# Layer 1's input of the next image loaded during layer 3, and its products and norms through single PSUM banks

## The chip, the cores and the metric

The kernel runs on one core of a Trainium2 chip, in one launch. The metric is the device time of that core in microseconds. The core has a matrix engine (TensorE, "PE" in the profile, whose weight loads are listed apart as "PEld"), a vector engine (VectorE, "DVE"), a scalar engine (ScalarE, "ACT"), a general engine (GpSimd, "POOL") and SyncE ("SP"), which issues DMA transfers. Matmul results go to PSUM, eight banks of 128 x 512 floats. All else that is worked on lies in SBUF. All data are fp32.

## The reference

Four images of 32 x 32 pixels (1024 tokens) with 384 channels pass through four residual layers, each after a group norm over 32 groups of 12 channels:

```python
x = x + layer0(gn(x)); x = x + layer1(gn(x)); x = x + layer2(gn(x)); x = x + layer3(gn(x))

# layer 0: deformable attention: q = x @ w_q, offsets by a grouped 3x3 convolution,
#   tokens sampled at shifted places, 6 heads of 64 with a sampled bias
# layer 1: attention with 12 heads of 32, weighted by how alike two tokens' groups are
qkv = x @ Wqkv                                       # -> q, k, v per head
xg  = x @ Wg + bg
gc  = depthwise_conv_3x3_stride2(xg, Wconv) + bconv  # 256 group centres
sim = sigmoid(beta + alpha * l2norm(xg_h) @ l2norm(gc).T)
group_weight = (sim @ sim.T) * gamma + (1 - gamma)
attn = softmax(q @ k.T * scale) * group_weight
attn = attn / (attn.sum(axis=2) + 1e-8)
out  = (attn @ v) @ Wproj
# layer 2: box sums over 5 columns and 20 channels, num / denum
# layer 3: outlook attention: v = x @ Wv; softmax over 9 for each of 9 window places of x @ Wa;
#   the weighted 3x3 patches are added back at their places
```

## The kernel before

An image is held channel-major: three tiles of 128 channels by 1024 tokens (`KC` = 3, `N` = 1024, `P` = 128; `NJ` = 8 blocks of 128 tokens). Layer 0 of an image is "the front" (class `Front`), layers 1 to 3 are "the trunk" (class `Trunk`, `image`). The front of image 1 runs alone. Then the trunk of image 1 runs beside the front of image 2 and so on, and the trunk of image 4 runs alone again. Both are generators: each `yield` gives a weight, and `Net.layer3` takes the next piece of the front whenever the front's share of work is less than 0.1 ahead of the trunk's. This sets the order in which the program is written; the order on each engine follows from a list scheduler when the kernel is built, and it is fixed then. Between front and trunk an image passes through DRAM (`self.x1`).

PSUM is split in two pools that front and trunk share: two "big" buffers of two banks (128 x 1024) and four single "bank" buffers (128 x 512). SBUF tiles come from pools with scopes: the tiles of a scope are given back at its end. Weights of 384 x 384 pass through a ring of three buffers (`weights`), loaded on SP's DMA queue, gmat (the group norm's averaging matrix) among them.

The places that the change touches, with the lines of the kernel before:

- `norm` (L309 to L357): the statistics of x on DVE (L306, L307), 14 matmuls with gmat that average the means (L330, from `gn_mv`), a few small DVE instructions, 14 matmuls for the deviations (L330, from `gn_d`), a square root, and three DVE instructions that write the normed x (L357).
- `inputs1` (L848 to L973), layer 1 up to its first head pair. It loads x (L852), norms it into xh, and makes three products with Wg (`dense_t`, L376, into a big buffer; bias on ACT, nine taps of the strided convolution on DVE). Then come the products for queries and keys (`queries_keys`, L885 to L893, six products into big buffers: queries evacuated by ACT, keys by DVE at L892, both stored to DRAM), the head norms (squares on ACT, matmuls with `hsum` L920, square root, reciprocal on DVE L934, broadcast back by `hall` matmuls at L947 into a big and a bank buffer, multiplied at L955 and L961) and the value products (`dense_n`, L390, a bank each, copied by ACT L899). Between these stand the eight steps of `sums_step` for the first pair: four matmuls (L1035) into both big buffers, a maximum on DVE (L1043) and an exponential with row sum on ACT (L1044), once for each of two heads. `sums_finish` (L1050 to L1063) takes the logarithm, transposes it and writes it to DRAM, from where `load_lse` brings it to a row of the query tile.
- `sims` (L1065 to L1087): eight matmuls (L1074) and four sigmoids (L1081) into a tile `sim`. `pair` then runs over eight blocks: POOL scales a block of sim (L1139), PE makes logits (L1154), ACT takes their exponential (L1162), and so on. In later pairs the sums of the following pair are made inside this loop.
- `layers23` and `layer2`: x comes back from DRAM on ACT's queue (L1227), and the denominators of layer 2 lie in three tiles `d`.
- The end of `layer3` (L1433 to L1481): for each of eight token blocks a row of DRAM is written (L1449) and read back shifted as `mt` (L1451), four on SP's queue and four on ACT's. PE meanwhile makes the last four value tiles (L390 from xh) and transposes x (24 transposes, L1460, three into each big buffer), which ACT copies into eight tiles y (L1464). Then come 22 products of `mt` and `vals` (L1472), the sum with y on DVE and the stores on SP (L1481).
- The front's instructions that stand around this place: its query product (L376 from `a`), the evacuation to `qpad` (L565), the convolution (L584) and, later, the indirect gathers that POOL issues (L652).

Of the kernel before, what the change touches and what calls it, by code (L numbers as in the profile page):

```python
# [26 lines left out]
P = 128  # L27
# [45 lines left out]
class Net:  # L73


    def __init__(self, ctx, tc, a):
        self.tc, self.nc, self.a = tc, tc.nc, a
        nc = self.nc
        pool = lambda name, bufs, **kw: ctx.enter_context(
            tc.tile_pool(name=name, bufs=bufs, **kw)  # L80
        )
        self.const = pool("const", 1)
        self.wts = pool("wts", 3)
        self.ps2 = pool("ps2", 2, space=PSUM)
        self.ps1 = pool("ps1", 4, space=PSUM)
        self.dram = pool("dram", 1, space=DRAM)
        self.n = 0
        self.consts()
        self.scratch()
        self.front, self.trunk = Front(self, "right"), Trunk(self, "left")  # L90

# [188 lines left out]
class Lane:  # L280
# [33 lines left out]
    def norm(self, x, out, mv=None):  # L314
# [7 lines left out]
        gmat = self.weights("gmat")  # L322
# [502 lines left out]
class Trunk(Lane):  # L825


    def image(self, b, out):
        with self.scope("l1y"):
# [18 lines left out]
    def inputs1(self, b):  # L848
        nc, v = self.nc, self.nc.vector
        x = self.wt([P, KC, N], "x")  # L850
        for k in range(KC):
            nc.sync.dma_start(x[:, k, :], self.x1[b % 2][k * P : (k + 1) * P, :])  # L852
        xh = self.wt([P, KC, N], "xh")
        self.norm(x, xh)
        yield 15

# [28 lines left out]
        def queries_keys(ko):  # L885
            for w, dst in ((wq, self.qd), (wk, self.kd)):
                ps = self.dense_t(w, xh, ko)
                t = self.wt([P, N], "qk", 2)
                if dst is self.qd:
                    nc.scalar.mul(t, ps, HD1**-0.5)  # L890
                else:
                    v.tensor_copy(t, ps)  # L892
                nc.sync.dma_start(dst[ko * P : (ko + 1) * P, :], t)  # L893
# [9 lines left out]
        queries_keys(0)  # L903
# [25 lines left out]
        queries_keys(1)  # L929
        yield 14  # L930
        wv = self.weights("Wqkv", 2 * C)
# [4 lines left out]
        queries_keys(2)  # L936
        yield 14
        self.sums_step(1, st)
        yield 10
        values(range(NJ // 2))  # L940
        self.sums_step(2, st)
        yield 18
        for k in range(KC):
            rows, heads = slice(k * P, (k + 1) * P), slice(32 * k, 32 * k + 32)
            ps, pc = self.big(), self.bank()
            for out, lo in ((ps[:, 0:512], 0), (ps[:, 512:N], 512), (pc[:, 0:M1], N)):
                nc.tensor.matmul(  # L947
                    out,
                    self.hall[heads, :],
                    inv[heads, lo : lo + out.shape[-1]],  # L950
                    start=True,
                    stop=True,
                )
            t = self.wt([P, N + M1], "sq", 2)
            v.tensor_tensor(  # L955
                t[:, 0:N].rearrange("p (y x) -> p y x", y=HW),
                pads[k][:, 1:, 1:],
                ps.rearrange("p (y x) -> p y x", y=HW),
                ALU.mult,
            )  # L960
            v.tensor_tensor(t[:, N:], raw[:, k, :], pc[:, 0:M1], ALU.mult)  # L961
# [4 lines left out]
            self.sums_step(3 + k, st)  # L966
            yield 8
        for i in range(2):
            values(range(4 + 2 * i, 6 + 2 * i))
            self.sums_step(6 + i, st)  # L970
        self.sums_finish(0, st)
        self.load_lse(0)
        yield 28  # L973
# [91 lines left out]
    def sims(self, p):  # L1065

        nc = self.nc
        sim = self.wt([P, 2, 2, N], "sim")
# [148 lines left out]
    def layers23(self, b, out):  # L1217
        with self.scope("l23"):
            self.x = self.wt([P, KC, N], "x")
# [36 lines left out]
    def layer2(self):  # L1256
        nc, v = self.nc, self.nc.vector
        with self.scope("l2"):
# [8 lines left out]
            def squares(k):  # L1267
# [24 lines left out]
                d = self.wt([P, HW, HW], "d", KC)  # L1292
# [61 lines left out]
    def layer3(self, b, out):  # L1354
        nc, v = self.nc, self.nc.vector
        skew = self.skew[b % 2]
        with self.scope("l3"):
# [98 lines left out]
            ys = []  # L1456
            for i in range(NJ):
# [5 lines left out]
                y = self.wt([P, C], "y", NJ)  # L1463
                nc.scalar.copy(y, pt[:, 0:C])  # L1464
                ys.append(y)
            yield 20
            for i in range(NJ):
# [11 lines left out]
                y = ys[i]  # L1479
# [87 lines left out]
```

## Time and profile before

| | |
|---|---|
| time, median of 3 runs | 4876.06 us (4868.23 to 4881.34) |
| the profiled execution's own time | 4831.1 us |
| its span, first to last instruction | 4829.3 us |
| granted TensorE clock, mean | 0.91 |
| front of image 1, alone | 0 to 637 us |
| trunk of images 1, 2, 3, 4 | 637 to 1829, to 2970, to 4055, to the end |
| PE, DVE, ACT, POOL busy | 87%, 65%, 50%, 20% |

The trunk's bounds are read from the last L1472 product of each image. The busy shares are means over stages that differ, so the stages that the change touches have to be read by themselves. PEclk is the mean clock that TensorE was granted in a stretch, as a share of full speed. The profile is of one execution and some 45 us below the median of the timed runs.

### The profile page before, as it was taken

To read this page: it belongs to the slowest core of one execution; us is meant where nothing else is said; L and a number is where in the kernel's file an instruction comes from. 1 tells how busy PE (TensorE), PEld (TensorE's weight loads), DVE (VectorE), ACT (ScalarE), POOL (GpSimd) and SP (SyncE) were. 2 spreads that over 40 slices of the span, in tenths; PEclk is the share of its full clock that TensorE was granted. 3 is DMA by queue.
4 is the path that set the end of the run, shared out by engine and by line. 5 is a ranking of instruction groups with operands and counts; after the bars stand their busy time and mean duration, and the time that the engine had idled before them with its cause. 6 is when DMAs were issued, how large, how long until landed. Compare 5 with 4: busy or idle time off the path is not lost.

```text
span 4829.3 us, 46659 instructions
## 1 busy us (share of the span) xinstructions
PE 4189.8 (87%) x15704; PEld 1799.4 (37%) x15704; DVE 3132.9 (65%) x5727; ACT 2404.9 (50%) x3693; POOL 946.3 (20%) x946
## 2 busy tenths in 40 slices
PE   5466678899999989889999989899999998999998
PEld 2222233333333353333333444343333335343444
DVE  3478828676877836577777762767687873454544
ACT  2155414565766513376666532457576641456642
POOL 1533303211212101421211210422121210000000
PEclk7677788999999989899999989799999998899998
DMA  6323244311212143431221224532121213201011
GB/s 118 102 84 92 70 131 144 94 53 38 80 50 73 36 147 105 126 86 50 60 62 54 65 76 113 154 92 56 33 80 42 75 45 114 87 23 33 19 39 40
DMA packets 230927, 366.82 MB, mean 76 GB/s; under 512 B 117475, under 2 KB 164672, under 8 KB 230688
## 3 DMA queue, kind: packets, MB, share of 16 engines
q1 hardware_dynamic: 169672, 197.36, 14.0%
q0 software_dynamic: 39936, 145.53, 10.3%
q10 hardware_dynamic: 21080, 20.96, 1.8%
q8 instruction: 124, 2.03, 0.2%
q14 instruction: 115, 0.94, 0.1%
HBM read 285.84 MB, written 78.21 MB: 75 GB/s over the span
## 4 chain that ended last, share of the span: by engine, by line
PE 35%; ACT 9%; DVE 7%; issue 3%; DMA 2%; POOL 0%; SPq 0%; ACTq 0%; DVEq 0%; POOLq 0%
PE bank L1184 8%; PE big L1154 4%; PE big L376 3%; PE big L1035 3%; PE bank L790 3%; PE bank L390 2%; PE bank L755 2%; PE bank L1128 2%; ACT big L1044 2%; PE bank L1179 2%; DVE e L1193 1%; DVE nmax L1043 1%; ACT e L1162 1%; PE big L1074 1%; PE bank L1472 1%
## 5 line engine op out<-in xcount | busy, mean ns | idle before, releaser
L1193 DVE SCALAR_TENSOR_TENSOR e<-bank,gam,e 128x512 f32<-128x512 f32 x768 | 557.6, 748 | 564.9 <-ACT gn L1192 275.1
L1184 PE MATMUL bank<-sim,sg 128*128 128x512 f32 (+3 forms) x2304 | 870.6, 512 | 2.8 <-DVE e L1193 2.8
L1044 ACT ACTIVATE big<-big,nmax 128x1024 f32<-128x1024 f32 x384 | 418.5, 1090 | 384.5 <-DVE nmax L1043 384.0
L734 POOL DMA_INDIRECT win<-strips,widx x384 | 425.8, 1109 | 887.4 <-DVE z L747 450.3
L1162 ACT ACTIVATE e<-big 128x1024 f32<-128x1024 f32 x384 | 376.8, 1019 | 360.2 <-PE big L1154 355.0
L1184 PEld LDWEIGHTS bank<-sim,sg 128*128 128x128 f32 x2304 | 405.9, 199 | 378.1 <-issue 297.7
L1043 DVE TENSOR_REDUCE nmax<-big 128x1 f32<-128x1024 f32 x384 | 453.1, 1217 | 54.4 <-PE big L1035 53.0
L1154 PE MATMUL big<-qa,ka 64*128 64x512 f32 x1536 | 412.1, 627 | 15.5 <-ACT big L1044 9.4
L1139 POOL TENSOR_SCALAR sg<-sim,gam 128x512 f32<-128x512 f32 x192 | 147.3, 770 | 1416.5 <-PE bank L1184 1126.9
L1035 PE MATMUL big<-k,q 32*128 32x512 f32 x1536 | 357.6, 701 | 74.5 <-ACT e L1162 37.0
L790 PE MATMUL bank<-lg,va 128*64 128x512 f32 x768 | 374.1, 634 | 44.7 <-ACT lg L788 44.6
L755 PE MATMUL bank<-qpad,kz 128*128 128x512 f32 x768 | 375.8, 620 | 22.6 <-DVE e L1193 13.7
L790 PE MATMUL bank<-lg,ones 128*64 128x512 f32 x768 | 373.4, 634 | 0.0
L746 ACT ACTIVATE z<-win,bias_f 128x528 f32<-128x528 f32 x384 | 277.0, 737 | 188.8 <-DVE lg L752 108.6
L752 DVE SCALAR_TENSOR_TENSOR lg<-z,bias_f,lg 128x512 f32<-128x512 f32 x384 | 299.9, 795 | 45.5 <-ACT lg L751 43.9
L747 DVE SCALAR_TENSOR_TENSOR z<-win,bias_f,z 128x528 f32<-128x528 f32 x384 | 291.8, 779 | 38.5 <-ACT z L746 38.1
L652 POOL DMA_INDIRECT gat<-pairs,sidx x192 | 210.8, 1098 | 448.1 <-DVE ix_gt L464 244.5
L751 ACT ACTIVATE lg<-z,bias_f 128x512 f32<-128x512 f32 x384 | 267.5, 719 | 44.1 <-DVE z L747 27.2
L787 DVE TENSOR_TENSOR lg<-lg,tb 128x512 f32<-128x512 f32 x384 | 246.2, 698 | 64.7 <-ACT tb L780 64.7
L756 DVE TENSOR_TENSOR lg<-bank,lg 128x512 f32<-128x512 f32 x384 | 256.3, 683 | 32.0 <-PE bank L755 30.7
L788 ACT ACTIVATE lg<-lg 128x512 f32<-128x512 f32 x384 | 222.4, 629 | 40.2 <-DVE lg L787 39.8
L1154 PEld LDWEIGHTS big<-qa,ka 64*128 64x128 f32 x1536 | 134.7, 188 | 272.0 <-issue 156.8
(262 smaller groups left out, 5812.2 us busy)
## 6 DMA issues: line engine op xcount, KB each, us to landing
pairs<-xn SPq DMA_DIRECT2D x64, 192.0 KB
q<-qd SPq DMA_DIRECT2D x48, 256.0 KB
w<-in_gmat SPq DMA_DIRECT2D x16, 576.0 KB
w<-in_w_off SPq DMA_DIRECT2D x12, 576.0 KB
w<-in_Wqkv SPq DMA_DIRECT2D x12, 576.0 KB
a<-in_x SPq DMA_DIRECT2D x16, 384.0 KB
x<-a ACTq DMA_DIRECT2D x4, 1536.0 KB
k<-a SPq DMA_DIRECT2D x12, 512.0 KB
```

Of the source, the lines that this page charges most:

```text
L734: nc.gpsimd.indirect_dma_start(out=win, out_offset=None, in_=self.strips[:, :], in_offset=bass.IndirectOffsetOnAxis(ap=self.widx[:, q, c : ...
L747: v.scalar_tensor_tensor(z, wv[:, 1 : HH + 1, 0 : HW + 1], sc(0, 1), z, ALU.mult, ALU.add)
L752: v.scalar_tensor_tensor(lg, z[:, :, 1 : HW + 1], sc(0, 0), lg, ALU.mult, ALU.add)
L755: nc.tensor.matmul(ps, kz[:, j * P : (j + 1) * P], both, start=True, stop=True)
L790: nc.tensor.matmul(po[out, :], w, lf, start=j == 0, stop=j == NJ - 1)
L1035: nc.tensor.matmul(ps[r][:, h * 512 : (h + 1) * 512], self.q4[rows, i * P : (i + 1) * P], self.k4[rows, 0:512], start=True, stop=True,)
L1043: v.tensor_reduce(nmax[:, r, i : i + 1], ps[r], AX.X, ALU.max, negate=True)
L1044: nc.scalar.activation(ps[r], ps[r], AF.Exp, bias=nmax[:, r, i : i + 1], accum_out=den[:, r, i : i + 1],)
L1154: nc.tensor.matmul(ps[:, r, :], ka[rows, j * P : (j + 1) * P], qa[rows, cols], start=True, stop=True,)
L1162: nc.scalar.activation(e, ps, AF.Exp)
L1184: nc.tensor.matmul(ps[:, (mid - i0) * P :], sg[:, r, m, :], sim[:, r, m, mid * P : i1 * P], start=m == 0, stop=m == 1,)
L1193: v.scalar_tensor_tensor(e[:, r, :], ps, self.gam[:, 1:2], e[:, r, :], ALU.add, ALU.mult, accum_out=tot[:, r, h : h + 1],)
```

## The change

The trunk gets a pool "keep" with one buffer of 128 x 4096 floats. `whole` hands it out: three quarters as x of an image, or all of it as the tile of `sims`, or three quarters as x of layers 2 and 3 and the fourth quarter as the third tile `d` of layer 2.

`start(b)` issues the loads of x and of gmat. For image 1 it is called at the head of `image`; for the others it is called in layer 3 of the image before, after the transposes of x (the buffer's last readers) and before the products with mt. The norm stands at the head of `image` and writes over x in place.

In layer 3 the eight tiles y are replaced by one tile that takes the place of xh, under the same tag.

`queries_keys` becomes `product`: each product is made in two halves, each in a bank, and evacuated by halves. The broadcast norms go through banks too, by 256, 512 and 512 columns. The order is rewritten: one product after each of the first sums steps, the sums steps 3 to 5 ahead of the norm of the same k, one value tile after each of the steps 3 to 7, the last three after `sums_finish`; the weights of the values are asked for later.

```diff
@@ -88,6 +88,7 @@
         self.consts()
         self.scratch()
         self.front, self.trunk = Front(self, "right"), Trunk(self, "left")
+        self.trunk.work = self.trunk.keep = pool("keep", 1, side="left")
 
     def nm(self, base):
         self.n += 1
@@ -311,7 +312,7 @@
         self.stat = self.work
         return self.wt([P, KC, 2], "gn_mv", 2)
 
-    def norm(self, x, out, mv=None):
+    def norm(self, x, out, mv=None, gmat=None):
 
 
         nc = self.nc
@@ -319,7 +320,8 @@
             mv = self.moments()
             for k in range(KC):
                 self.stats(mv, x, k)
-        gmat = self.weights("gmat")
+        if gmat is None:
+            gmat = self.weights("gmat")
 
         near = [[k for k in range(KC) if abs(k - ko) <= 1] for ko in range(KC)]
 
@@ -825,7 +827,28 @@
 class Trunk(Lane):
 
 
+    def whole(self):
+
+
+        work, self.work = self.work, self.keep
+        t = self.wt([P, 4 * N], "whole")
+        self.work = work
+        return t, t[:, 0 : KC * N].rearrange("p (k n) -> p k n", k=KC)
+
+    def start(self, b):
+
+        x = self.whole()[1]
+        for k in range(KC):
+            self.nc.sync.dma_start(x[:, k, :], self.x1[b % 2][k * P : (k + 1) * P, :])
+        self.begun = x, self.weights("gmat")
+
     def image(self, b, out):
+        if b == 0:
+            self.start(b)
+        x, gmat = self.begun
+        self.norm(x, x, None, gmat)
+        self.xh = x
+        yield 15
         with self.scope("l1y"):
 
 
@@ -847,13 +870,7 @@
 
     def inputs1(self, b):
         nc, v = self.nc, self.nc.vector
-        x = self.wt([P, KC, N], "x")
-        for k in range(KC):
-            nc.sync.dma_start(x[:, k, :], self.x1[b % 2][k * P : (k + 1) * P, :])
-        xh = self.wt([P, KC, N], "xh")
-        self.norm(x, xh)
-        yield 15
-
+        xh = self.xh
 
         pads, raw = [], self.wt([P, KC, M1], "raw")
         w = self.weights("Wg")
@@ -882,15 +899,24 @@
 
         wq, wk = self.weights("Wqkv"), self.weights("Wqkv", C)
 
-        def queries_keys(ko):
-            for w, dst in ((wq, self.qd), (wk, self.kd)):
-                ps = self.dense_t(w, xh, ko)
-                t = self.wt([P, N], "qk", 2)
+        def product(w, ko, dst):
+
+            t = self.wt([P, N], "qk", 2)
+            for h in range(2):
+                ps, out = self.bank(), t[:, h * 512 : (h + 1) * 512]
+                for ki in range(KC):
+                    nc.tensor.matmul(
+                        ps,
+                        w[:, ki, ko * P : (ko + 1) * P],
+                        xh[:, ki, h * 512 : (h + 1) * 512],
+                        start=ki == 0,
+                        stop=ki == KC - 1,
+                    )
                 if dst is self.qd:
-                    nc.scalar.mul(t, ps, HD1**-0.5)
+                    nc.scalar.mul(out, ps, HD1**-0.5)
                 else:
-                    v.tensor_copy(t, ps)
-                nc.sync.dma_start(dst[ko * P : (ko + 1) * P, :], t)
+                    v.tensor_copy(out, ps)
+            nc.sync.dma_start(dst[ko * P : (ko + 1) * P, :], t)
 
         def values(js):
             for j in js:
@@ -900,7 +926,9 @@
                 nc.sync.dma_start(self.vd[j * P : (j + 1) * P, :], t)
 
 
-        queries_keys(0)
+
+        product(wq, 0, self.qd)
+        product(wk, 0, self.kd)
         self.load_sums(0)
         self.load_pair(0)
         st = self.sums_state()
@@ -926,50 +954,49 @@
                 )
         nc.scalar.activation(inv[:, 0:N], psx[0 : KC * 32, :], AF.Sqrt)
         nc.scalar.activation(inv[:, N:], psc[0 : KC * 32, 0:M1], AF.Sqrt)
-        queries_keys(1)
+        product(wq, 1, self.qd)
         yield 14
-        wv = self.weights("Wqkv", 2 * C)
         for part in (inv[:, 0:512], inv[:, 512:]):
             v.tensor_scalar(part, part, 1e-12, None, ALU.max)
             v.reciprocal(part, part)
         self.sums_step(0, st)
-        queries_keys(2)
+        product(wk, 1, self.kd)
         yield 14
         self.sums_step(1, st)
-        yield 10
-        values(range(NJ // 2))
+        product(wq, 2, self.qd)
+        wv = self.weights("Wqkv", 2 * C)
+        yield 14
         self.sums_step(2, st)
-        yield 18
+        product(wk, 2, self.kd)
+        yield 14
         for k in range(KC):
+            self.sums_step(3 + k, st)
             rows, heads = slice(k * P, (k + 1) * P), slice(32 * k, 32 * k + 32)
-            ps, pc = self.big(), self.bank()
-            for out, lo in ((ps[:, 0:512], 0), (ps[:, 512:N], 512), (pc[:, 0:M1], N)):
+            t = self.wt([P, N + M1], "sq", 2)
+            parts = [(N, M1, raw[:, k, :], t[:, N:])]
+            for h in range(2):
+                out = t[:, h * 512 : (h + 1) * 512].rearrange("p (y x) -> p y x", x=HW)
+                parts.append((h * 512, 512, pads[k][:, 1 + 16 * h : 17 + 16 * h, 1:], out))
+            for at, n, src, out in parts:
+                ps = self.bank()[:, 0:n]
                 nc.tensor.matmul(
-                    out,
-                    self.hall[heads, :],
-                    inv[heads, lo : lo + out.shape[-1]],
-                    start=True,
-                    stop=True,
-                )
-            t = self.wt([P, N + M1], "sq", 2)
-            v.tensor_tensor(
-                t[:, 0:N].rearrange("p (y x) -> p y x", y=HW),
-                pads[k][:, 1:, 1:],
-                ps.rearrange("p (y x) -> p y x", y=HW),
-                ALU.mult,
-            )
-            v.tensor_tensor(t[:, N:], raw[:, k, :], pc[:, 0:M1], ALU.mult)
+                    ps, self.hall[heads, :], inv[heads, at : at + n], start=True, stop=True
+                )
+                if at < N:
+                    ps = ps.rearrange("p (y x) -> p y x", x=HW)
+                v.tensor_tensor(out, src, ps, ALU.mult)
             nc.sync.dma_start(self.xgd[rows, :], t[:, 0:N])
             nc.sync.dma_start(self.gcd[rows, :], t[:, N:])
             if k == 0:
                 self.load_groups(0)
-            self.sums_step(3 + k, st)
+            values(range(k, k + 1))
             yield 8
         for i in range(2):
-            values(range(4 + 2 * i, 6 + 2 * i))
             self.sums_step(6 + i, st)
+            values(range(3 + i, 4 + i))
         self.sums_finish(0, st)
         self.load_lse(0)
+        values(range(5, NJ))
         yield 28
 
     def pair_tiles(self):
@@ -1065,7 +1092,7 @@
     def sims(self, p):
 
         nc = self.nc
-        sim = self.wt([P, 2, 2, N], "sim")
+        sim = self.whole()[0].rearrange("p (r m n) -> p r m n", r=2, m=2)
         for h in range(2):
             for m in range(2):
                 ps = self.big().rearrange("p (r n) -> p r n", r=2)
@@ -1216,7 +1243,8 @@
 
     def layers23(self, b, out):
         with self.scope("l23"):
-            self.x = self.wt([P, KC, N], "x")
+            whole, self.x = self.whole()
+            self.spare = whole[:, KC * N :].rearrange("p (y x) -> p y x", y=HW)
             yield from self.out1(b)
             yield from self.layer2()
             yield from self.layer3(b, out)
@@ -1289,7 +1317,7 @@
                 nc.scalar.activation(s, ps, AF.Square)
                 num.append(s)
                 t = self.wt([P, HW, HW + 2], "t", 2)
-                d = self.wt([P, HW, HW], "d", KC)
+                d = self.wt([P, HW, HW], "d", 2) if k < 2 else self.spare
                 v.tensor_tensor(t, sq[:, :, 0 : HW + 2], sq[:, :, 1 : HW + 3], ALU.add)
                 v.tensor_tensor(d, t[:, :, 0:HW], t[:, :, 2 : HW + 2], ALU.add)
                 v.tensor_tensor(d, d, sq[:, :, 4 : HW + 4], ALU.add)
@@ -1453,17 +1481,19 @@
                 )
 
             values(range(NJ // 2, NJ))
-            ys = []
+
+            ys = self.wt([P, KC, N], "xh").rearrange("p k (a c) -> p (k a) c", c=P)
+            ys = ys.rearrange("p (i k) c -> p i (k c)", k=KC)
             for i in range(NJ):
                 pt = self.big()
                 for k in range(KC):
                     nc.tensor.transpose(
                         pt[:, k * P : (k + 1) * P], self.x[:, k, i * P : (i + 1) * P], self.ident
                     )
-                y = self.wt([P, C], "y", NJ)
-                nc.scalar.copy(y, pt[:, 0:C])
-                ys.append(y)
+                nc.scalar.copy(ys[:, i], pt[:, 0:C])
             yield 20
+            if b + 1 < NB:
+                self.start(b + 1)
             for i in range(NJ):
                 ps = self.bank()
                 near = [j for j in range(NJ) if abs(i - j) <= 1]
@@ -1476,7 +1506,7 @@
                         start=j == near[0],
                         stop=j == near[-1],
                     )
-                y = ys[i]
+                y = ys[:, i]
                 v.tensor_tensor(y, ps[:, 0:C], y, ALU.add)
                 nc.sync.dma_start(out[i * P : (i + 1) * P, :], y)
                 yield 4
```

## The prediction

> **What bounds the kernel now.** I read the shares and the chain first: TensorE (PE) is busy 87% of the span and leads the chain that ended last, with ACT and DVE behind it. A change pays where PE waits or where its granted clock (PEclk) is low. The edits touch two places, layer 3's end and layer 1's inputs, so I cut these out as time windows.
>
> ```profile
> span 4829.3 us, 46659 instructions
> PE 4189.8 (87%) x15704; PEld 1799.4 (37%) x15704; DVE 3132.9 (65%) x5727; ACT 2404.9 (50%) x3693; POOL 946.3 (20%) x946
> ```
>
> Windows (after the time: busy us per engine, PEclk, DMA share, GB/s). The first three are image 2's start, with image 3's front beside it; the rest is image 4's start, with nothing beside it. The columns to read are PE busy and PEclk: 0.62 at the norm, 0.73 and 0.50 at the sums.
>
> ```profile
> 1828.00:1853.00 25.00, 21.03 (x100) 9.60 (x92) 7.70 (x18) 1.54 (x2) 8.22 (x16) 0.66 0.29 103
> 1926.00:1974.00 48.00, 41.57 (x108) 16.64 (x107) 34.64 (x33) 18.60 (x33) 37.38 (x35) 0.68 0.60 187
> 1974.00:1990.00 16.00, 9.31 (x26) 3.58 (x26) 9.93 (x10) 8.90 (x13) 10.41 (x9) 0.57 0.78 205
> 4054.00:4072.00 18.00, 7.06 (x30) 6.27 (x28) 5.98 (x16) 1.55 (x2) 8.21 (x16) 0.62 0.29 109
> 4139.00:4178.00 39.00, 33.48 (x92) 12.67 (x90) 18.82 (x18) 14.98 (x27) 0.00 (x0) 0.73 0.26 88
> 4178.00:4190.00 12.00, 8.06 (x17) 2.48 (x19) 0.19 (x2) 7.86 (x11) 1.36 (x2) 0.50 0.58 159
> ```
>
> The timeline of image 4's start (start, duration, engine, line; in brackets the idle before and who ended it):
>
> ```profile
> 4041.46 13.07 PE L1472 MATMUL bank<-vals,mt 128*128 128x384 f32 x40
> 4063.00 0.55 PE L330 MATMUL bank<-gn_mv,w 128*128 128x1 f32 x2 [8.47 <-DVE gn_mv L307]
> 4067.91 3.15 PE L330 MATMUL bank<-gn_d,w 128*128 128x1 f32 x14 [0.84 <-DVE gn_d L347]
> 4072.47 27.40 PE L376 MATMUL big<-xh,w 128*128 128x512 f32 x60 [1.41 <-DVE xh L357]
> 4170.70 2.35 DVE L1043 TENSOR_REDUCE nmax<-big 128x1 f32<-128x1024 f32 x2 [3.65 <-PE big L1035]
> 4174.41 1.14 PE L1035 MATMUL big<-k,q 32*128 32x512 f32 x8
> 4175.66 2.35 DVE L1043 TENSOR_REDUCE nmax<-big 128x1 f32<-128x1024 f32 x2 [2.60 <-PE big L1035]
> 4190.07 2.67 PE L1154 MATMUL big<-qa,ka 64*128 64x512 f32 x8
> ```
>
> The first line is the end of image 3, at 4054.5.
>
> **The change, part by part.**
>
> *Image 4's boundary, nothing beside it.* From 4054.5 to 4072.5 PE does only the norm: 18.0 us. With x and its statistics there already, what is left is the chain behind them: the mean matmuls 3.15 (14 as in the row at 4067.91), 0.84 on DVE, the deviation matmuls 3.15, 1.41 to the first xh: 8.55 us. Saved 18.0 - 8.55 = 9.4. The three x loads are issued on SP behind the first y store and wait for the last transpose; their cover is layer 3's 13 us run of products (4041.5 to 4054.5), and a load takes about 4 us from issue (SP 4057.3, statistics 4061.3), so they hide; without cover the 9.4 is lost. What queues behind them on SP is seven y stores, which nothing waits for, and at images 1 and 2 two conv weight tiles of the front, which were ahead of the y stores. I put the x loads there at 1798; 1.5 MB of x and 0.6 MB of weights at the 185 GB/s of the stretch 1773 to 1805 land by 1810, and the second L584 group (72 matmuls are two groups), behind transposes, L376, the first group and five products, comes at about 1816: nothing, by 6 us; without that cover up to 5 each.
>
> *Image 4's inputs to the first logits, 4072.5 to 4190.1: 117.6 us.* PE work at the durations of full-clock rows: nine products of 12 matmuls at 27.40/60 = 0.457, 49.3, eight value tiles 15.7, head sums 4.9, broadcasts 6, sums 8 x 1.14 = 9.1, sims 4.2: 89 us. Now the sums steps, the query/key products and three norm tiles share two big PSUM buffers: each sums step holds both through reduction and exponential, and the next product waits. A step takes 4.95 us from reduction to reduction, with PE mostly idle in it. Afterwards only the sums use the big pair; products and norms have small banks, and fill the steps. So two chains compete: PE's 89 us plus fill and drain, and the sums chain. The latter: the norms' reciprocals end on DVE 44 us after the first Wg product (4108.68 + 8.15); eight steps of 5 give 84; finish, and sims with its table load, as now 14 from the last sums matmul (4175.6 to 4190.1): 98. I take 101, a saving of 16.6. The bounds: 5 (the steps stretch to 6.5, because value copies and halves of evacuations stand in ACT's and DVE's order between them) and 22 (all at full clock). Evacuating in halves costs more calls: two of about 0.6 for one of 1.02 (ACT) or 1.23 (DVE), some 1.5 us in all on engines that are at most half busy here. The sims no longer wait for the lse transfer (2.17 us before ACT at 4183.94), but three value tiles, 6 us of PE, now stand ahead of them under that wait: nothing either way. The value weights are asked for later, still two steps ahead of the first value tile, some 10 us for a load of about 5. The buffer that x, the sims and layer 2's x now share is rewritten only after readers that the program's order puts well ahead: nothing.
>
> *Images 2 and 3.* The front covers the boundary: PE idles 4 us ahead of the norm (1828 to 1853), and then runs at half clock. 25.6 us would be 14.7 with no hole and full clock: 10.9 saved. The stretch 1853 to 1990 has some 17 us of idle PE and the low clock of the rows above. But on POOL 48 gathers of the front run from 1919.9 to 1990.0, and the first pair's scaling (L1139) stands behind them in both kernels:
>
> ```profile
> 1919.87 1.07 POOL L652 DMA_INDIRECT gat<-pairs,sidx  x1 [80.97 <-DVE ix_gt L464]
> 1980.66 2.22 POOL L652 DMA_INDIRECT gat<-pairs,sidx  x1 [3.45 <-DVE xn L668]
> 1990.03 1.37 POOL L1139 TENSOR_SCALAR sg<-sim,gam 128x512 f32<-128x512 f32 x2
> ```
>
> So what is saved ahead moves the gathers earlier, and the rest stays hidden: I take the boundary's 10.9 plus 3 for the stretch (bounds 0 and 12), less the stall below, 7.5: 6.5 for each image.
>
> *Image 1* has no prefetch; its stretch also ends at POOL: 4 saved (0 to 9).
>
> *Layer 3's end, the cost.* The y tiles now lie in xh, so their copies wait until the last value tile has read xh; and in ACT's order all eight copies stand behind its four mt loads, which wait for the skewed rows to land. Before, three or all of them were ahead. Behind the mt issues on ACT also stands the front's qpad evacuation:
>
> ```profile
> 1783.33 5.19 ACTq L1451 DMA_DIRECT2D mt<-skew  x4
> 1787.00 8.32 PE L376 MATMUL big<-a,w 128*128 128x512 f32 x19
> 1792.35 1.12 ACT L565 ACTIVATE qpad<-big,cols 128x1024 f32<-128x1024 f32 x1 [12.08 <-DMA mt<-skew]
> 1797.39 7.96 PE L584 MATMUL big<-qpad,w 64*64 64x512 f32 x72
> 4810.32 0.88 PE L1472 MATMUL bank<-vals,mt 128*128 128x384 f32 x2 [2.33 <-DMA mt<-skew]
> ```
>
> On PE, the front's L376 and L584 work, which filled this wait at the end of images 1 and 2, now stands behind the transposes and the first three products. From the last value tile (about 1785) to the first copy (1792) PE has only two tiles of transposes: 7 us idle, and the pairs of transposes then go at the pace of the copies. Here a rule speaks against the change. The row: the 4 us hole at 1832 left PEclk 0.66, while one of 2.05 us at 4037 left 1.00. The Trainium skill, "TensorE: Matmul & The Clock Gate", Part 1 (The HAM clock gate), says that an idle window of about 3.4 us halves the clock, and that about as long a busy stretch brings it back. By the row of the short hole the stall costs 7 us; by the rule 7 plus 3.4 us of work at half speed, about 1.7 more. If, as in 1926 to 1974, the clock stays low (0.68) while work is broken up, the 16 us of L376 and L584 add up to 8. I take 7.5. At the ends of images 3 and 4 the hole is 2.3 us and grows to about 3: 1 us each, up to 6 with the clock lost over the 13 us run.
>
> **The sum.** Image 4: -9.4 - 16.6 = -26. Images 2 and 3: -13. Image 1: -4, less the end of image 1, which is in image 2's account. Ends of images 3 and 4: +2. Together -41 on the profiled 4831.1 (span 4829.3 and 1.8 around it): 4790. The median of the runs is 4876.06, 45 above that execution; I carry the difference over: 4876 - 41 = 4835.
>
> **Rivals.** *Only image 4 gains (chance 0.22):* the POOL gathers hide all of the gain beside the front, as the row at 1990.03 allows; the stall eats the boundary. -26 + 5: 4855. Against it: PE itself idles at the boundary. *More (0.17):* with the holes gone the clock holds in 1926 to 1990 too (64 us at 0.65, of which some 15 each would come back), image 4 takes its 22: about -75, 4801. Against it: the gathers keep their pace. *The layer-3 stall decides (0.08), slower:* one mechanism, the y copies behind the mt loads on ACT. It has to cost more than 41 + 15 in all four ends, so 22 at each of images 1 and 2 and 8 at 3 and 4 on top of what I took: qpad waits for eight copies, L584 for qpad, and the front's chain moves back by as much: 4893. Against it: all mt loads have landed by 1794, so it can hardly exceed 15. *It doesn't do what it says (0.10):* x is prefetched, but the sums chain at 5 us a step bounds the inputs as before, and the boundary's gain pays the stall: -9 + 0: 4867.
>
> **How the numbers follow.** My case has 0.43, with its own range 4818 to 4850. Within 0.3% (14.6 us, about what a measurement can tell) is the last rival and part of the first's upper edge: 0.12; slower 0.08; faster 0.80. The range for 8 in 10 runs from the larger gain to the smallest: 4798 to 4870.
>
> **What would show it.** Right: the boundary 4054 to 4072 shrinks to about 9 us with no 8.47 wait on the statistics; the first L1154 of image 4 comes about 101 us after its first Wg product, with PEclk near 1.00 in between; in layer 3 of images 1 and 2, 7 us of idle PE ahead of the first mt product. Wrong: sums steps of 6 us or more, ACT's first y copy much after the last mt issue, the front's L584 later by over 15 us, or pair 0 of images 2 and 3 still starting behind gathers that came no earlier.

## The result, and the profile after

The changed kernel takes 4825.04 us (median of five runs, 4816.15 to 4828.93) against 4871.16 us for the kernel before (five runs, 4860.06 to 4881.34): a ratio of 0.9902, 95% interval 0.9887 to 0.9918. It was measured twice more, each time beside the kernel before: 0.9885 and 0.9891. The forecast was 4835, a gain of 41; measured were 46, 56 and 53 (the last two worked out as 1 less the ratio, times 4834.78 and 4831.27).

The profiled execution of the changed kernel, its page:

```profile
span 4827.1 us, 46697 instructions
PE 4154.0 (86%) x15704; PEld 1782.7 (37%) x15704; DVE 3134.6 (65%) x5751; ACT 2407.5 (50%) x3705; POOL 948.4 (20%) x946
```

Its span is only 2 us below that of the first profile of before, though the times differ by 46. One trace is one execution, and this one has waits beside the front which a second trace lacks (they stand at the end of this text). Image 4, which has no front beside it, is alike in all traces of one kernel, so it is read first.

Image 4 in the first trace of the changed kernel, as windows (columns as before: time, busy us of PE, PEld, DVE, ACT, POOL, PEclk, DMA share, GB/s), then its PE timeline:

```profile
4080.00:4088.00 8.00, 5.01 (x30) 4.70 (x28) 2.98 (x8) 0.26 (x1) 4.27 (x5) 0.67 0.24 67
4088.00:4139.00 51.00, 50.95 (x126) 20.56 (x127) 29.60 (x40) 15.16 (x21) 5.47 (x12) 0.95 0.29 98
4139.00:4178.00 39.00, 36.94 (x127) 15.96 (x126) 21.80 (x26) 21.26 (x38) 0.00 (x0) 1.00 0.50 162
4178.00:4187.00 9.00, 6.93 (x22) 2.74 (x22) 0.00 (x0) 5.74 (x6) 1.36 (x2) 0.90 0.54 162
```

```profile
4080.24 1.62 PE L332 MATMUL bank<-gn_mv,w 128*128 128x1 f32 x14
4082.70 3.15 PE L332 MATMUL bank<-gn_d,w 128*128 128x1 f32 x14 [0.84 <-DVE gn_d L349]
4088.05 18.13 PE L378 MATMUL big<-whole,w 128*128 128x512 f32 x36 [2.20 <-DVE whole L359]
...
4153.61 1.14 PE L1062 MATMUL big<-k,q 32*128 32x512 f32 x8
4154.58 2.31 PE L982 MATMUL bank<-inv,hall 32*128 32x256 f32 x6
4156.82 2.20 PE L392 MATMUL bank<-w,whole 128*128 128x384 f32 x6
4158.95 1.14 PE L1062 MATMUL big<-k,q 32*128 32x512 f32 x8
...
4187.26 2.67 PE L1181 MATMUL big<-qa,ka 64*128 64x512 f32 x8
```

The norm's matmuls follow at once on layer 3's last product, with no 8.47 us wait for the statistics: the boundary is 7.65 us (4080.4 to 4088.05) where it was 18.0. In the sums, PE is busy for 36.9 of 39 us at full clock where it had 33.5 at 0.73. A sums step, a norm and a value tile follow each other without a hole, 5.3 us a round. From the first Wg product to the first logits it takes 99.2 us instead of 117.6, and PE is busy for 94.8 of the 99 us from 4088 to 4187.

For images 1 to 3 I compare the first trace of before with the second of the changed kernel (run e5 below, span 4777.7), since neither has the unexplained waits; their difference, 51.6 us, agrees with the ratios. Times in us:

| | before | changed |
|---|---|---|
| image 1: to first logits / from there to layer 3's end | 216.7 / 974.1 | 215.5 / 981.9 |
| image 2: the same | 162.3 / 977.5 | 144.3 / 985.5 |
| image 3: the same | 162.8 / 924.1 | 143.9 / 926.1 |
| image 4: the same | 135.5 / 635.6 | 105.5 / 634.4 |

The left number starts at the end of layer 3's last product of the image before (637 for image 1). In the first trace of before these ends are 1827.8, 2967.6 and 4054.5; the bounds of the trunk given ahead of the prediction are 0.5 to 2.4 us too late. The gains are at the left: 18.0, 18.9 and 30.0 at images 2 to 4. The cost is at the right: 7.8, 8.0 and 2.0 at images 1 to 3. Cut from the first value tile of layer 3 (L390 before, L392 after) to the last product, images 1 and 2 take 84.4 and 85.3 us instead of 77.5 and 76.8, with PE idle for 6.2 and 6.9 instead of some 1.5, so the cost lies there. For image 1 only the sum of the two numbers is firm: 1191 before, 1197 here, and 1196 in a third trace of the changed kernel, which splits it into 210.0 and 986.1.

Windows of image 2 in that second trace, then POOL's first gather and the first pair's scaling, then the end of image 1:

```profile
1834.00:1849.00 15.00, 15.00 (x109) 7.34 (x108) 5.23 (x9) 1.53 (x3) 9.74 (x16) 1.00 0.31 93
1849.00:1915.00 66.00, 59.85 (x167) 24.47 (x165) 60.12 (x115) 30.86 (x48) 3.44 (x4) 0.92 0.28 93
1915.00:1979.00 64.00, 50.00 (x147) 22.04 (x149) 43.27 (x58) 27.37 (x45) 50.56 (x47) 0.76 0.64 200
```

```profile
1910.65 0.99 POOL L654 DMA_INDIRECT gat<-pairs,sidx  x1 [63.44 <-DVE sidx L496]
1978.02 1.37 POOL L1166 TENSOR_SCALAR sg<-whole,gam 128x512 f32<-128x512 f32 x2
```

```profile
1785.41 0.55 PE L1490 MATMUL big<-ident,whole 128*128 128x128 f32 x3 [0.81 <-ACT xh L1493]
1789.15 1.62 PE L1502 MATMUL bank<-vals,mt 128*128 128x384 f32 x2 [3.19 <-DMA mt<-skew]
1790.56 1.49 PE L1490 MATMUL big<-ident,whole 128*128 128x128 f32 x6
...
1795.47 10.46 PE L378 MATMUL big<-a,w 128*128 128x512 f32 x24
1805.86 7.96 PE L586 MATMUL big<-qpad,w 64*64 64x512 f32 x72
```

The boundary of image 2 (15 us) has no idle PE and full clock, where 25 us at 0.66 stood. The gathers start 76.3 us after layer 3's end (1834.36) instead of 92.1, and the scaling stands at 143.7 instead of 162.2: they moved forward with the rest. From the first gather to the scaling it is 67.4 us instead of 70.2, and POOL has no gap of more than 0.31 us in it. In layer 3's end PE waits for mt, the matmuls behind it run at half clock (six transposes in 1.49 us, which take 0.82 at the end of image 4), and the front's L378 and L586, which filled this place in the kernel before, come after.

### The profile page after: what moved, and what is told of

Its sections match the earlier page's. It is cut to its first block, busy times and chain, and to the rows that moved or that the text cites. A ratio compares the mean times of both kernels' runs of the same rounds, so it can differ in the third digit from the quotient of the medians.

```text
span 4827.1 us, 46697 instructions
## 1 busy us (share of the span) xinstructions
PE 4154.0 (86%) x15704; PEld 1782.7 (37%) x15704; DVE 3134.6 (65%) x5751; ACT 2407.5 (50%) x3705; POOL 948.4 (20%) x946
## 3 DMA queue, kind: packets, MB, share of 16 engines
q1 hardware_dynamic: 169672, 197.36, 13.9%
q0 software_dynamic: 39936, 145.53, 10.3%
## 4 chain that ended last, share of the span: by engine, by line
PE 35%; ACT 8%; DVE 8%; issue 3%; DMA 2%; POOL 0%; SPq 0%; ACTq 0%; DVEq 0%; POOLq 0%
PE bank L1211 8%; PE big L1181 4%; PE big L1062 3%; PE bank L792 2%; PE bank L757 2%; PE bank L392 2%; PE bank L1155 2%; PE bank L1206 2%; ACT big L1071 2%; PE big L378 2%; DVE e L1220 1%; DVE nmax L1070 1%; PE big L1334 1%; PE bank L1502 1%; ACT e L1189 1%
## 5 line engine op out<-in xcount | busy, mean ns | idle before, releaser
L1211 PE MATMUL bank<-whole,sg 128*128 128x512 f32 (+3 forms) x2304 | 867.2, 510 | 3.5 <-DVE e L1220 3.5
L1211 PEld LDWEIGHTS bank<-whole,sg 128*128 128x128 f32 x2304 | 403.6, 198 | 377.7 <-issue 297.3
L1166 POOL TENSOR_SCALAR sg<-whole,gam 128x512 f32<-128x512 f32 x192 | 147.7, 772 | 1395.8 <-PE bank L1211 1136.3
L1062 PE MATMUL big<-k,q 32*128 32x512 f32 x1536 | 332.8, 686 | 94.5 <-ACT big L1071 41.2
L1181 PEld LDWEIGHTS big<-qa,ka 64*128 64x128 f32 x1536 | 135.5, 188 | 273.8 <-issue 154.9
```

Source lines behind the costliest of these rows:

```text
L1062: nc.tensor.matmul(ps[r][:, h * 512 : (h + 1) * 512], self.q4[rows, i * P : (i + 1) * P], self.k4[rows, 0:512], start=True, stop=True,)
L1181: nc.tensor.matmul(ps[:, r, :], ka[rows, j * P : (j + 1) * P], qa[rows, cols], start=True, stop=True,)
L1211: nc.tensor.matmul(ps[:, (mid - i0) * P :], sg[:, r, m, :], sim[:, r, m, mid * P : i1 * P], start=m == 0, stop=m == 1,)
```

## The experiments

Each was timed beside the kernel before; ratios are to it, and stretches are read from the traces.

**A second trace of the kernel before (e1).** No edit.

> The kernel before, unchanged, for a second trace. The first one lies 40 us below the median of the timed runs, while the changed kernel's lies 4 above its own, so the two traces alone show a gain of 2 us where the times show 46. Theory A (the gain lies in image 4 and in images 1 to 3): a trace of a usual execution, near 4870, has image 4 at 771 us as before (771.2 in the first) and the missing 40 us in images 1 to 3, whose last product then ends near 4095 instead of 4054.5. Theory B (the first trace is usual and the gain is image 4's 28 us alone): this one ends again near 4830, with images 1 to 3 at 4054 within 10.

Ratio 1.000 (0.9983 to 1.0017), median 4858.53 (4841.88 to 4878.45 in 12 runs); span of the trace 4851.8. Image 4 takes 771.0, as before (771.2); images 1 to 3 end at 4077.3, 23 us later than in the first trace, 17 of them in image 3. Theory A holds as far as it goes: the variation lies beside the front, and the first trace of before is one of the shorter executions. It does not account for the whole 40 us.

**The call of the prefetch moved back (e2).**

```diff
-        if b == 0:
-            self.start(b)
+        self.start(b)
...
-            if b + 1 < NB:
-                self.start(b + 1)
```

> The changed kernel with the prefetch alone undone: x and the group matrix are asked for at the head of each image. By my account of the prediction the prefetch gives 9.4 us at image 4 and 11 at each of images 2 and 3, less the cost of a load moved past the y stores: 25 to 31 us slower than the changed kernel, near 4853. If the front hides the boundary at images 2 and 3, only image 4's part is lost: 9 us, near 4834.

Ratio 0.9918 (0.9898 to 0.9938). The edit did not do what it was meant to: in the trace the x loads of image 4 are issued at 4055.8, 12 us ahead of layer 3's end (4068.0), as in the changed kernel. The scheduler sends them as soon as the buffer is free. What makes the prefetch is the buffer, not the place of the call.

**The prefetch alone (e3).** The shared buffer, the prefetch and the y tiles in xh as changed; all of `inputs1` from the query products on as before.

```diff
-        def product(w, ko, dst):
+        def queries_keys(ko):
...
```

> The kernel before with the shared buffer, the prefetch and the y tiles in xh, but its own products, norms and order up to the first pair. By the prediction's account: 9.4 at image 4 and 22 less 15 of stall at images 2 and 3, less 2 at the ends: 14 us faster than before, near 4857. If the boundary's gain is eaten by the stall: no faster than 9, and image 4's way to the first logits as before, 117.6 us from its first Wg product.

Ratio 0.9992 (0.9977 to 1.0007): 4 us faster, not distinguishable from nothing; 14 had been forecast. In the trace image 4's boundary and inputs take 125.0 us against 136.7 in the trace of before at its side. At images 2 and 3 the first sums step comes 11.6 and 12.1 us earlier after the boundary, but from there to the first logits it takes 97.8 and 107.0 us instead of 90.6 and 101.8: about half of the gain is given back among the sums. (Image 3 has an unexplained wait in that stretch in both traces, so its split is rough; image 2 has none.) The forecast had 17 us of cost at layer 3's ends; cut as above, from the first value tile, the four ends are 7.5, 8.4, 3.2 and 4.3 us longer than in the trace of before at its side.

**Six of the eight y tiles in a buffer of their own,** twice (e4, e11).

```diff
-            ys = self.wt([P, KC, N], "xh").rearrange(...)
+            own = self.wt([P, 6, C], "ys")
+            late = self.wt([P, KC, N], "xh")[:, 0, 0 : 2 * C].rearrange("p (i c) -> p i c", c=C)
+            ys = [own[:, i] for i in range(6)] + [late[:, i] for i in range(2)]
```

> The changed kernel with six of the eight y tiles in a buffer of their own, so that their copies stand ahead of the mt loads on ACT again (the last two stay in xh). If the stall at the y copies costs what I put on it, 7.5 us at each of images 1 and 2 and 1 at images 3 and 4: up to 17 us faster than the changed kernel, near 4808. If transposes only fill a wait for mt that is there anyway: within 5 of it.

> Six y tiles in their own buffer again, now beside the changed kernel on the same chip. The first trace of it had PE wait 6.4 us for the first mt with no transposes left to fill the wait, where the changed kernel waits 3 to 4 and then transposes. If the stall in layer 3 is the copies behind the mt loads: 10 to 17 us faster than the changed kernel. If it is the wait for mt itself, with the front's matmuls no longer in it: within 5.

Ratios 0.9902 (0.9878 to 0.9926), and 0.9900 (0.9885 to 0.9915) beside 0.9891 for the changed kernel: within 5 us of it. The end of image 1 in the second trace:

```profile
1777.74 7.91 PE L392 MATMUL bank<-w,xh 128*128 128x384 f32 x24
1791.08 1.62 PE L1503 MATMUL bank<-vals,mt 128*128 128x384 f32 x2 [5.44 <-DMA mt<-skew]
1792.50 11.34 PE L378 MATMUL big<-a,w 128*128 128x512 f32 x24
```

The six copies now stand ahead of the mt loads on ACT, and the hole is still there, 5.4 us instead of 3.2 and 0.8 with a few transposes around. So the copies behind the mt loads cost nothing that shows: the hole is the wait for mt itself. That the front's matmuls no longer lie in it can be seen in both orders; no run put them back, and why the scheduler places them later stays open.

**The changed kernel again,** as the measure of its neighbours, twice (e5, e9).

> The changed kernel, unchanged, for a second trace and as the measure of the three beside it. The ratio to the kernel before is 0.990 again (0.9902 in the first). In the trace image 4 takes 743 us from the end of image 3's products, as in the first (743.1); if images 1 to 3 together lie 10 us or more off the first trace's 3443, what the two first traces showed there is chance of one execution and not the change.

> The changed kernel unchanged, as the measure of the three beside it: ratio to the kernel before 0.988 to 0.991.

Ratios 0.9885 (0.9869 to 0.9902) and 0.9891 (0.9874 to 0.9909); spans 4777.7 and 4782.6. Image 4 takes 739.9 and 742.4 (743.1 in the first trace), images 1 to 3 together 3397 and 3400 instead of 3443. The first trace's 46 us there are of that execution, not of the change.

**The prefetch undone (e6),** by keeping the buffer in use until the end of layer 3.

```diff
-            for i in range(NJ):
-                pt = self.big()
+            def turned(i):
+                pt = self.big()
...
+            for i in range(NJ - 1):
+                turned(i)
...
+                if i == NJ - 1:
+                    turned(i)
                 y = ys[:, i]
```

> The changed kernel with the prefetch really undone: the transposes of the last token block are made after the products instead of before them, so that the buffer of x comes free, and the loads start, some 2 us before layer 3's end instead of 12. (To move the call of start alone had left the loads in place, since the scheduler issues them as soon as the buffer is free.) If the early loads are worth what I forecast at image 4 (9.4) and the front hides the rest: 8 to 10 us slower than the changed kernel, all of it between the last product and the first Wg product. If also the forecast for images 2 and 3 holds: 20 to 30 slower.

Ratio 0.9946 (0.9929 to 0.9963) beside 0.9885: 30 us slower by the ratios. Image 4's boundary:

```profile
4063.89 0.59 PE L332 MATMUL bank<-gn_mv,w 128*128 128x1 f32 x2 [5.41 <-DVE gn_mv L308]
4067.49 2.83 PE L332 MATMUL bank<-gn_mv,w 128*128 128x1 f32 x12 [3.02 <-DVE gn_mv L308]
4071.17 3.15 PE L332 MATMUL bank<-gn_d,w 128*128 128x1 f32 x14 [0.84 <-DVE gn_d L349]
4075.82 6.42 PE L378 MATMUL big<-whole,w 128*128 128x512 f32 x8 [1.50 <-DVE whole L359]
```

The waits for the statistics are back, and from layer 3's end to the first logits it takes 117.2 us instead of 105.5 here, 154.3 and 154.2 instead of 144.3 and 143.9 at images 2 and 3. So in the changed kernel the early loads are worth 10 to 12 us at each boundary, with a front beside it or without. The ends of images 1 and 2 take 84.5 and 83.9 us from the first value tile here, as in the changed kernel: the cost at layer 3's end does not come from the early loads.

**The query and key products back in big buffers (e7).**

```diff
-            for h in range(2):
-                ps, out = self.bank(), t[:, h * 512 : (h + 1) * 512]
...
+            ps = self.dense_t(w, xh, ko)
+            t = self.wt([P, N], "qk", 2)
...
```

> The changed kernel with the query and key products back in big buffers, whole; order, norms and prefetch as changed. If the shared big pair is what slowed the sums, four of the six products fall among the first three sums steps and each takes a buffer for about 3 us: image 4 10 to 14 us longer before its first logits. If the order is what counts: within 4.

Ratio 1.0023 (1.0016 to 1.0030): the whole gain is gone, 67 us, and more than the expectation: 17.4 us at image 4, 11.9, 15.8 and 16.2 at images 1 to 3 before the first logits. Image 4, PE and then DVE:

```profile
4149.54 1.45 PE L973 MATMUL bank<-inv,hall 32*128 32x256 f32 x4
4151.01 7.11 PE L378 MATMUL big<-whole,w 128*128 128x512 f32 x12
4158.05 2.31 PE L1053 MATMUL big<-k,q 32*128 32x512 f32 x8
...
4161.80 7.11 PE L378 MATMUL big<-whole,w 128*128 128x512 f32 x12 [0.59 <-ACT big L1062]
```

```profile
4147.30 1.22 DVE L909 COPY qk<-big 128x1024 f32<-128x1024 f32 x1 [8.03 <-PE big L378]
4159.22 2.41 DVE L1061 TENSOR_REDUCE nmax<-big 128x1 f32<-128x1024 f32 x2 [7.32 <-PE big L1053]
```

Sums step and product alternate in the two big buffers. A product waits for an exponential, PE falls to a lower clock (7.11 us for 12 matmuls, against 5.42 for 12 of the products in the changed kernel), and the reductions of the next step wait 7.3 us for PE. One round of sums step and product takes 10.8 us; in the changed kernel the rounds with 12 or more matmuls of a product take 7.3 to 7.5. Beside the front the sums hold up the gathers too. POOL at image 2:

```profile
1927.11 1.07 POOL L654 DMA_INDIRECT gat<-pairs,sidx  x1 [64.14 <-DVE ix_gt L466]
1959.73 2.22 POOL L654 DMA_INDIRECT gat<-pairs,sidx  x1 [10.28 <-DVE xn L670]
2000.29 2.22 POOL L654 DMA_INDIRECT gat<-pairs,sidx  x1 [6.10 <-DVE xn L670]
2009.92 1.36 POOL L1157 TENSOR_SCALAR sg<-whole,gam 128x512 f32<-128x512 f32 x2
```

The gathers start 77.0 us after the boundary, as in the changed kernel (76.3), but reach the scaling 82.8 us later instead of 67.4. For 17.4 of these POOL waits for DVE to empty a gathered tile (xn), which stands behind reductions that wait for PE in DVE's order.

**The broadcast norms back in big buffers (e8).**

```diff
-                ps = self.bank()[:, 0:n]
+            ps, pc = self.big(), self.bank()
```

> The changed kernel with the broadcast norms back in big buffers; the rest as changed. If the shared pair counts: three tiles, each 3 us of a buffer in steps 3 to 5 of the sums, 8 to 10 us longer in image 4. If only the order counts: within 4. Beside the front (images 1 to 3) either way no more than 5 each, if the gathers set the pace there.

Ratio 0.9953 (0.9937 to 0.9970), 33 us slower than the changed kernel by the ratios, 25 between the two traces: 8.6 at image 4, as expected, and 1.8, 7.1 and 7.9 at images 1 to 3, where I had put 5 at most.

**The order of before, with prefetch and small banks (e10).**

```diff
         product(wq, 1, self.qd)
+        product(wk, 1, self.kd)
...
         self.sums_step(0, st)
-        product(wk, 1, self.kd)
+        product(wq, 2, self.qd)
+        product(wk, 2, self.kd)
...
-            values(range(k, k + 1))
```

> The changed kernel with prefetch and small banks for products and norms, but the order of the kernel before around the sums (both products of a k together, four value tiles ahead of step 2, pairs of value tiles at the end). If the banks are what counts (undoing them for the products cost 66 us and for the norms 31): within 8 us of the changed kernel. If the order gives the gain and the banks only allow it: 20 to 40 slower.

Ratio 0.9928 (0.9913 to 0.9943) beside 0.9891: 12 us slower by the medians, 18 by the ratios, 14 between the traces; 8.2 of it at image 4 and 8.1 at image 2. That lies between the two expectations: with the banks in place the order is worth something beside them, and less than they are.

**An attempt at a faster one (e12):** six y tiles of their own, and the first sums step ahead of the reciprocals.

```diff
+        self.sums_step(0, st)
         for part in (inv[:, 0:512], inv[:, 512:]):
             v.tensor_scalar(part, part, 1e-12, None, ALU.max)
             v.reciprocal(part, part)
-        self.sums_step(0, st)
```

> An attempt at a faster one: six y tiles of their own, and the first sums step ahead of the reciprocals (8.15 us on DVE) instead of behind them. If DVE's order holds up the first sums beside the front (PE waits 2.8 and 5.1 us there for the first two steps' exponentials): 5 to 15 us faster than the changed kernel, in images 1 to 3. If the gathers or TensorE set the pace: within 4.

Ratio 0.9907 (0.9892 to 0.9922), beside 0.9891: no gain. No version beat the changed kernel.

## Why the prediction was right

The time, 4825, lies in the range, and the gain is between 1.1 and 1.4 times the forecast. Some 5 of the 10 us between 4825 and 4835 are the base, whose median was 4871 here and not 4876. What carries over is the gain: beside kernels of before at 4835 and 4831, the changed kernel took 4779 and 4784, below the range's end at 4798. By its steps, measured between the first trace of before and the second of the changed kernel:

| step | forecast | measured |
|---|---|---|
| image 4, boundary | -9.4 | -11.2 (18.0 to 6.8) |
| image 4, inputs to the first logits | -16.6 | -18.9 (117.6 to 98.7) |
| images 2 and 3, boundary and stretch, each | -13.9 | -18.0 and -18.9 |
| ends of images 1 and 2, the stall | +7.5 each | +7.8 and +8.0 |
| image 1, to the first logits | -4 | -1.2 |
| ends of images 3 and 4 | +1 each | +2.0 and -1.2 |
| sum | -41 | -51.6 |

*Image 4* went as worked out. The norm's chain of 8.55 us was 6.8 here and 7.65 in the first trace, since the mean matmuls run at full clock when they follow without a hole (1.62 us for 14). The inputs took 99 where I took 101: with banks of their own the products fill the sums steps, and PE, busy for 94.8 of the 99 us in the first trace, sets the time. The runs e7 and e8 show that each of the two uses of banks is needed; taken back singly they cost 17 and 9 us at this place.

*Images 2 and 3* gained more than I said, 18.0 and 18.9 for 13.9, and both terms of that sum were too small. In this pair the boundary gave 13.7 and 13.9 (25.6 and 25.8 to 11.9) where I took 10.9, and the stretch 4.3 and 5.1 where I took 3. In the third trace of the changed kernel, where 68 matmuls of the front at image 2's boundary take 9.64 us instead of 7.94, it is 12.0 and 12.2, then 6.5 and 3.7. That what is saved ahead moves the gathers earlier is what happened: they start 15.8 us sooner after the boundary, and 11.6 of that comes with the early loads alone (e3, 80.1 us, against e1, 91.7). That the rest stays hidden held in size: the stretch of the gathers is only 2.8 us shorter, and PE is still idle for 14 of the 64 us of the window beside them, where it was 13. What I did not see is that this cover has no pace of its own. It runs without a wait only as long as DVE empties its tiles in time, and with the products back in the big pair it took 82.8 us (e7). The first rival, that only image 4 gains, falls with the gathers' earlier start.

*The stall* has the size I gave it, but not the cause, and its size is in part luck. I put it on the y copies behind the mt loads; with six of them moved ahead of the loads the time is the same. The early loads are not the cause either (e6), nor the rewritten inputs, since e3 has it without them (85.0 and 84.9 us from the first value tile). The hole is the wait for mt (3.2 us here, and 0.8 ahead of it), followed by some 5 us at half clock, and what was lost is, as far as the two orders show, the front's work that had lain in it. PE's idle time grew by about 5 us instead of 7, and the half clock made up the rest. The slow rival, that this stall decides, had the same mechanism and falls too: cut from the first value tile, no end in this trace or the third lost more than 9.

*The larger gain* was half right. The clock at the boundary came back in full (1.00 from 0.66), and beside the gathers only from 0.65 to 0.76. *That the sums chain bounds the inputs as before* describes the prefetch alone (e3, 0.9992), not the change.

The account was a sum of parts. Taken in one order the parts add up: with the loads late (e6) the first logits of images 4, 2 and 3 come 18.3, 8.0 and 8.6 us sooner than in the kernel before, and the early loads add 11.7, 10.0 and 10.3. In the other order they do not: in e3 the early loads bring 11.7 at image 4 and only 4.4 and 6.9 at images 2 and 3, where the sums still wait for the big pair. And the three parts taken back singly cost 30, 67 and 33, together far more than the gain.

## What to carry to other kernels

Where a chain of short steps holds a small pool of PSUM buffers through reduction and exponential, give the independent matmuls that are to fill its waits a pool of their own; sharing costs both sides, and the new order with the products still in the shared pair was no faster than the kernel before (e7). The order with no other part was not tried. With a list scheduler like this one a load starts when its buffer comes free (e2, e6), so ask who is the buffer's last reader, not where the call stands. And single traces of one kernel can differ by as much as the change (4827.1 and 4777.7 here): read a stage that nothing disturbs, or take a second trace.

## What was not expected of the hardware

*Waits that nothing in the profile explains.* In the first trace of the changed kernel, at image 2, ACT and DVE stand still for 12.4 and 10.3 us while the front's gathers run. ACT, then DVE:

```profile
1958.53 0.19 ACT L1071 ACTIVATION_READ_ACCUMULATOR big<-big,nmax 128x1 f32 x1
1971.09 0.48 ACT L925 COPY vn<-bank 128x384 f32<-128x384 f32 x1 [12.37 <-remote]
```

```profile
1968.06 0.56 DVE L670 TENSOR_TENSOR xn<-gat 128x384 f32<-128x384 f32 x1
1978.89 2.35 DVE L1070 TENSOR_REDUCE nmax<-big 128x1 f32<-128x1024 f32 x2 [10.28 <-remote]
```

The matmuls that both need had ended by 1960.3, and no engine is named as releaser. Waits of over 6 us on ACT without a named releaser sum to 8.3 to 21.5 us in five of the fourteen traces, the first of the changed kernel and e1 to e4, and to none in the nine others. What holds the engines stays open; no run was made for it. The kernel before was slower beside the runs that show them (medians 4871 and 4856, then 4835 and 4831), while the ratio of the changed kernel stayed between 0.9885 and 0.9902.

*The length of a hole does not decide the clock.* In the second trace of the changed kernel a hole of 1.89 us at the end of image 3 is followed by half clock, in the first one a hole of 2.58 us at the end of image 4 is not. The second trace, then the first:

```profile
4016.09 1.07 PE L1502 MATMUL bank<-vals,mt 128*128 128x384 f32 x2 [1.89 <-DMA mt<-skew]
4016.95 1.49 PE L1490 MATMUL big<-ident,whole 128*128 128x128 f32 x6
```

```profile
4807.09 0.88 PE L1502 MATMUL bank<-vals,mt 128*128 128x384 f32 x2 [2.58 <-DMA mt<-skew]
4807.81 0.82 PE L1490 MATMUL big<-ident,whole 128*128 128x128 f32 x6
```

Six transposes take 1.49 us in the one and 0.82 in the other. The Trainium skill, "TensorE: Matmul & The Clock Gate", Part 1 (The HAM clock gate), has the clock watched in windows of 3.4 us that run freely, not from the hole's start. That would let equal holes end differently, and the clock records bear it out: in each of the fourteen traces all changes of the granted clock lie on one grid of 3.41 us. The hole of 1.89 us falls whole into one cell of it, with PE busy for 1.41 of the 3.30 us from 4013.3 on, and PEclk is 0.50 from 4016.7 to 4020.0. The hole of 2.58 us is cut by a cell's edge at 4806.35 into 1.84 and 0.74; PE is busy for 1.51 of the 3.30 us from 4803.0 on, and PEclk stays 1.00.

But a hole of 1.89 us is well short of an idle window of 3.4, so the figure does not hold as a bound here. Of the 16195 cells at full clock in the fourteen traces, all 600 with PE busy below 40% were followed by half clock, and so were 284 of the 788 between 40 and 60% (by the profile's modelled ends of matmuls). From half clock, no cell with PE busy below 79% was followed by full clock (0 of 1511). What decides between 40 and 60% is not shown. What a hole costs hangs on where it falls in the grid, so my price for the stall could be right only as a mean.
